# Two moves in a two-layer conv and attention kernel: which engine evicts q and k in the first part, and when the banded conv weights are zeroed

## The chip, the cores and the metric

The kernel runs on one core of one Trainium2 chip. The metric is the device time of one execution in microseconds (us). The time before is the median of three runs; the profile is of one further execution.

## The reference, cut to what matters

The input x is (2, 256, 64, 64): two images of 256 channels, 4096 tokens each. Two layers follow each other.

```python
# layer 0: attention over all 4096 tokens, 8 heads of 32 channels
q, k, v = proj(Wq, bq) / sqrt(32), proj(Wk, bk), proj(Wv, bv)   # 1x1 convolutions
attn = softmax(q @ k.T); fuse = attn @ v
x = conv1x1(concat([x, fuse]), Wf, bf) * m + x * (1 - m)        # m: mask, resized
# layer 1: channel gate, attention in 8x8 windows, two grouped 7x7 convolutions as a gate
x = x * sigmoid(relu(x @ ca_w1 + ca_b1) @ ca_w2 + ca_b2)
x = x + window_attention(x)
x = shuffle(x)                                                   # channels of 4 groups interleaved
y = relu(bn1(conv7x7(x, sa_w1)))                                 # 64 groups of 4 channels
y = bn2(conv7x7(y, sa_w2))
return x * sigmoid(y)
```

## The kernel before, in words

The program has three parts.

**The first part** (L366 to L512) makes q, k and v of all 16 chunks (2 images by 8 chunks of 512 tokens) and writes them to DRAM. A first loop (L420) takes a chunk at a time: TensorE makes q and then k, each a PSUM pair of two banks of 128 x 512 (L432, three such pairs in rotation). Each bank is read twice. VectorE adds the bias into an SBUF tile, `qst` or `kst` (L442), and ScalarE writes the square of the same sum to `sq` (L443). SyncE's queue stores `qst` and `kst` to DRAM (L447, L450); each of these tiles has two buffers. VectorE then takes the maximum over groups of four tokens of the squares (`top4`, L451), and TensorE sums them over the channels of a head one chunk later (`nrm`, L412), from which a flag is made that chooses between two versions of the attention. A second loop (L464) makes v of each chunk, ScalarE evicts it (L477), and GpSimd's queue stores it (L482).

Beside these loops runs `prepare`, a generator that the first part steps once per chunk. It builds the mask and the folded weights of the two convolutions on VectorE and, at its end, fills `w_s` with zeros: `w_s` is a DRAM tensor of 16 groups by 128 rows by 1792 floats (896 KB a group), and each group is one transfer on GpSimd's queue from a zeroed SBUF tile (L327), four of them to a step.

**The attention** (`pipeline`, L521) goes through 1024 slots in an order written out by hand: image, chunk of queries, group of four heads, block of 128 keys. In a slot TensorE makes four score tiles (L630) of the slot two ahead and four products with v (L659), ScalarE takes exponentials (L640), and VectorE adds the 128 x 2048 exponentials to a running sum for the denominators (L661). k and v come back from DRAM in pieces of four slots on SyncE's queue (`ka`, L557; `va`, L559), asked for two pieces ahead into three buffers. After each chunk of queries a generator `stage` (L718) does the rest of layer 0 and layer 1's window attention in small steps, one every fourth slot, and ends with stores of its rows to a DRAM tensor `x_s` on GpSimd's queue (L976).

`bands` (L338) is a third generator. It writes the weights' rows from two small DRAM tensors (`r1_s`, `r2_s`) into the diagonals of the zeroed `w_s`, in 156 small transfers on GpSimd's queue (L347, L353, L361), one each sixth slot. The slots only fix where these stand in the order of GpSimd's queue. Nothing in that queue waits for the attention before the first stores of `x_s`, so GpSimd issues what stands ahead of them as fast as its own waits for earlier transfers let it.

**The convolutions** (`convolve`) read `w_s` (from the last chunk of queries on) and `x_s`, and write the output.

Of the kernel before, what the change touches and what calls it, by code (L numbers as in the profile page):

```python
# [10 lines left out]
F32 = mybir.dt.float32  # L11
I32 = mybir.dt.int32
AF = mybir.ActivationFunctionType
# [6 lines left out]
P = 128  # L20
KC = C // P
# [25 lines left out]
NU = NG // UG  # L47
UW = UG * KS
# [7 lines left out]
def conv_seq_kernel(ctx: ExitStack, tc: tile.TileContext, a, out):  # L56
    nc = tc.nc
    const = ctx.enter_context(tc.tile_pool(name="const", bufs=1))
    dram = ctx.enter_context(tc.tile_pool(name="dram", bufs=1, space=bass.MemoryType.DRAM))
# [11 lines left out]
    def psum2(name):  # L71
        return ps["pair"].tile([P, 2, CH], F32, tag="s", name=name)

    def psum1(name):
        return ps["one"].tile([P, CH], F32, tag="h", name=name)
# [50 lines left out]
    w_s = dram.tile([NU, P, 2 * 32 * UW], F32, name="ws")  # L126
# [29 lines left out]
    for h in range(2):  # L156
        pending.append((cb1[64 * h : 64 * h + 64], a["ca_b1"]))
        pending.append((cw2[64 * h : 64 * h + 64], a["ca_w2"]))

    r1_s = dram.tile([32 + 4, NU, UW], F32, name="r1s")  # L160
    r2_s = dram.tile([32 + 4, NU, 4, UW // 4], F32, name="r2s")

# [2 lines left out]
    def prepare(mk, cwp):  # L165
# [55 lines left out]
        zero = cwp.tile([P, 2 * 32 * UW], F32, name="zero")  # L221
# [50 lines left out]
        for name, t in (  # L272
# [4 lines left out]
            g, beta, mean, var, cbias = (t[:, :, i] for i in range(5))  # L277
# [28 lines left out]
        for i in range(4):  # L306
            h, k = i % 2, i // 2
# [15 lines left out]
        nc.gpsimd.dma_start(  # L323
            r2_s.rearrange("p u i f -> p (u i f)"), m2.rearrange("p u i q x -> p (u i q x)")
        )
        for u in range(NU):
            nc.gpsimd.dma_start(w_s[u], zero)  # L327
            if u % 4 == 3:
                yield

    def spread(row, n):
        f = row.shape[-1]
        return row.rearrange("p u f -> u p f").to_broadcast([NU, n, f])


    def bands():  # L338
        band1 = w_s.rearrange("u p (m f) -> u (p m) f", f=UW)
        band2 = w_s.rearrange("u p (m f) -> u (p m) f", f=UW // 4)  # L340
        for q in range(4):
            for dy in range(KS):
                r0, r1 = max(0, dy - PAD), min(RB, RB + dy - PAD)
                p0, m0, n = 32 * q + 1 + r0, 1 + r0 - dy + PAD, r1 - r0
                k = KS * q + dy
                at0, step = p0 * 64 + m0, 64 + 1
                nc.gpsimd.dma_start(  # L347
                    band1[:, at0 : at0 + step * (n - 1) + 1 : step, :], spread(r1_s[k : k + 1], n)
                )
                yield  # L350
                for i in range(4):
                    at0, step = p0 * 256 + 128 + i * 32 + m0, 256 + 1
                    nc.gpsimd.dma_start(  # L353
                        band2[:, at0 : at0 + step * (n - 1) + 1 : step, :],
                        spread(r2_s[k : k + 1, :, i], n),
                    )
                    yield
            for i in range(4):
                at0 = 32 * q * 256 + 128 + i * 32 + 1
                nc.gpsimd.dma_start(  # L360
                    band2[:, at0 : at0 + RB, :], spread(r2_s[32 + q : 33 + q, :, i], RB)  # L361
                )
                yield
# [5 lines left out]
    with (  # L369
# [8 lines left out]
        for n in ("WqT", "WkT", "WvT"):  # L378
            t = w0.tile([P, KC, C], F32, name=n)
# [3 lines left out]
        bias = {}  # L383
        for n in ("bq", "bk"):
            t = w0.tile([P, KC], F32, name=n)
# [11 lines left out]
        def load_chunk():  # L397
            if len(xs0) == len(chunks):
                return
            b, c = chunks[len(xs0)]  # L400
            x = x0.tile([P, KC, CH], F32, name=f"x0_{b}_{c}")
            src = a["x"][b].rearrange("(k p) h w -> p k (h w)", p=P)
            nc.sync.dma_start(x, src[:, :, c * CH : (c + 1) * CH])
            xs0.append(x)
# [3 lines left out]
        def norms(i, tops):  # L408
            s = psum1(f"nrm_{i}")
            for n in range(2 * KC):  # L410
                s_ = s[32 * n : 32 * n + 32, 0 : CH // 4]
                nc.tensor.matmul(s_, headsum, tops[:, n, :], start=True, stop=True)  # L412
            nc.vector.tensor_reduce(nm[:, i : i + 1], s[:, 0 : CH // 4], AX.X, ALU.max)

        prepared = prepare(mk, cwp)
        next(prepared)
        for _ in range(3):
            load_chunk()
        last = None
        for i, (b, c) in enumerate(chunks):  # L420
            load_chunk()
            x = xs0[i]
            sq = st0.tile([P, 2 * KC, CH], F32, tag="sq", name=f"sq_{b}_{c}")
            tops = st0.tile([P, 2 * KC, CH // 4], F32, tag="top4", name=f"top4_{b}_{c}")
            for n, w in (("q", wq), ("k", wk)):
                s = psum2(f"{n}0_{b}_{c}")
                for g in range(KC):
                    for kc in range(KC):
                        rhs = x[:, kc, :]
                        if n == "q":  # L430
                            rhs = rhs.rearrange("p (r w c) -> p w r c", r=WS, w=NW)
                        nc.tensor.matmul(  # L432
                            s[:, g, :],
                            w[:, kc, g * P : (g + 1) * P],
                            rhs,
                            start=(kc == 0),
                            stop=(kc == KC - 1),
                        )
                t = st0.tile([P, KC, CH], F32, tag=n, name=f"{n}st_{b}_{c}")
                bt = bias["b" + n]  # L440
                for g in range(KC):
                    nc.vector.tensor_scalar_add(t[:, g, :], s[:, g, :], bt[:, g : g + 1])  # L442
                    nc.scalar.activation(  # L443
                        sq[:, g + KC * (n == "k"), :], s[:, g, :], AF.Square, bias=bt[:, g : g + 1]
                    )
                if n == "q":
                    nc.sync.dma_start(q_s[b, c], t.rearrange("p g n -> p (g n)"))  # L447
                else:
                    for g in range(KC):
                        nc.sync.dma_start(k_s[b, g, c], t[:, g, :])  # L450
            nc.vector.tensor_reduce(  # L451
                tops, sq.rearrange("p g (n f) -> p g n f", f=4), AX.X, ALU.max
            )
            if i:
                norms(i - 1, last)
            last = tops
            for t, src in pending[4 * i : 4 * i + 4]:
                nc.scalar.dma_start(t, src)
            next(prepared, None)
# [4 lines left out]
        for i, (b, c) in enumerate(chunks):  # L464
            s = psum2(f"v0_{b}_{c}")
# [30 lines left out]
            elif i == 2:  # L496


                s = psum1("bvf")
# [21 lines left out]
    def pipeline(arm, shifted, pools):  # L521
# [25 lines left out]
        def at(delay, action):  # L547
            later.append((now[0] + delay, action))

        def load_piece(n):  # L550
            if n * PB >= len(slots):
                return
            b, c, g, m = slots[n * PB]
            p = m // PB
            nm_ = f"{arm}_{b}_{c}_{g}_{p}"
            k = kvp.tile([P, PB * P], F32, tag="k", name=f"k{nm_}")
            nc.sync.dma_start(k, k_s[b, g, p])  # L557
            v = kvp.tile([P, PB, P], F32, tag="v", name=f"v{nm_}")
            nc.sync.dma_start(v, v_s[b, g, p].rearrange("p (m d) -> p m d", m=PB))  # L559
            kts[b, c, g, p], vts[b, c, g, p] = k, v  # L560

        def load_q(b, c):
            q = qp.tile([P, KC, CH], F32, tag="q", name=f"q{arm}_{b}_{c}")
            nc.sync.dma_start(q, q_s[b, c].rearrange("p (g n) -> p g n", g=KC))
            qts[b, c] = q
# [571 lines left out]
        def run_later():  # L1137
            for _ in range(len(later)):
                due, action = later.popleft()
                if due <= now[0]:  # L1140
                    action()
                else:
                    later.append((due, action))
# [8 lines left out]
        banded = bands()  # L1152
# [8 lines left out]
        for i, (b, c, g, m) in enumerate(slots):  # L1161
            now[0] = i
            if (b, c, g, m) == (B - 1, NCHUNK - 1, 0, 0):
                conv = convolve()
                next(conv)
            if m % PB == 0:
                load_piece(i // PB + AHEAD)
            if g == KC - 1 and m == 0:
                nxt = (b, c + 1) if c + 1 < NCHUNK else (b + 1, 0)
                if nxt[0] < B:  # L1170
                    load_q(*nxt)
            rest = scores(i + 2) if i + 2 < len(slots) else None
            products(i)
            if rest:
                rest()
            if g == KC - 1 and m == NMB - 1:
                at(DN + 5, lambda b=b, c=c: stages.append(stage(b, c)))
            run_later()
            if i % 6 == 1:
                next(banded, None)  # L1180
            if i % 4 == 0:
                run_stages()
# [102 lines left out]
```

## Time and profile before

| what | us |
|---|---|
| median of three runs | 3063.85 (3060.79 to 3065.46) |
| the profiled execution, its own time | 3056.05 |
| its span in the profile | 3054.1 |
| TensorE busy | 2973.5 |
| VectorE busy | 2543.1 |
| ScalarE busy | 2449.0 |
| GpSimd busy | 358.5 |

The span starts with the first instruction. In it the first part takes the first 218 us, the attention runs from there to about 2810 us, and the convolutions take the rest. A busy share is a mean over these three; what an edit is worth has to be read from the stage that it is in. In lines of the profile PE is TensorE, PEld its weight load, DVE is VectorE, ACT ScalarE, POOL GpSimd and SP SyncE; a "q" behind an engine marks the DMA issues of its queue, `q0` is the DMA queue that GpSimd's issues feed, and `q1` that of SyncE's.

### The profile page before, as it was taken

The numbers are of one execution on the slowest core, as the hardware profiler recorded it, in microseconds if no ns is written. First come the engines' busy times: TensorE is split into PE (matmuls) and PEld (weight loads), VectorE is DVE, ScalarE is ACT, GpSimd is POOL, SyncE is SP. The second block draws the span as 40 slices with busy tenths as digits, with TensorE's granted clock in tenths as the row PEclk, the third lists the DMA queues.
The fourth block names the chain that finished last, engine by engine and source line by source line (L and its number), as shares of the span: only waits on it lengthen the run. The fifth ranks groups of instructions, "written<-read, shape, count | busy, mean of one in ns | idle before, by whom it ended". The sixth has DMA issues, their size and how long they took to land.

```text
span 3054.1 us, 60829 instructions
## 1 busy us (share of the span) xinstructions
PE 2973.5 (97%) x25114; PEld 1007.6 (33%) x25114; DVE 2543.1 (83%) x1411; ACT 2449.0 (80%) x4115; POOL 358.5 (12%) x617
## 2 busy tenths in 40 slices
PE   8899989999999999999999999999999999999997
PEld 3372222232322222222222222222222222233675
DVE  5519989999999999898999998999999998999111
ACT  2239979898989899898989898989898998988333
POOL 8130000001010101010100001010101010000256
PEclk9999999999999999999999999999999999999998
DMA  7854212324242424242322324232424242413364
GB/s 214 322 176 79 63 51 63 68 60 73 62 77 60 67 73 73 66 67 74 62 72 60 66 60 73 60 74 60 75 65 70 67 70 71 105 57 106 99 196 106
DMA packets 158703, 264.19 MB, mean 87 GB/s; under 512 B 44424, under 2 KB 63068, under 8 KB 158416
## 3 DMA queue, kind: packets, MB, share of 16 engines
q1 hardware_dynamic: 129056, 213.33, 25.3%
q0 software_dynamic: 24800, 44.16, 9.3%
q8 instruction: 200, 3.28, 0.5%
q10 hardware_dynamic: 4560, 2.70, 0.3%
q14 instruction: 87, 0.71, 0.1%
HBM read 197.89 MB, written 65.21 MB: 86 GB/s over the span
## 4 chain that ended last, share of the span: by engine, by line
PE 82%; DVE 6%; ACT 2%; DMA 2%; POOL 1%; issue 0%; SPq 0%; DVEq 0%
PE sa L630 34%; PE ava L659 31%; DVE suma L661 5%; PE qka L800 4%; PE hya L729 4%; PE c2a L1064 2%; PE vwa L886 2%; PE opa L950 2%; PE c1a L1040 1%; ACT ea L640 1%; POOL out_dram L1096 1%; PE sca L834 1%; PE rda L697 1%; PE ca2a L772 1%; PE pta L909 1%; PE oa L928 1%
## 5 line engine op out<-in xcount | busy, mean ns | idle before, releaser
L661 DVE TENSOR_TENSOR suma<-suma,ea 128x2048 f32<-128x2048 f32 x960 | 2198.5, 2290 | 86.8 <-ACT ea L640 3.9
L640 ACT ACTIVATE ea<-sa 128x512 f32<-128x512 f32 (+1 forms) x3072 | 2043.9, 745 | 85.6 <-PE sa L630 40.2
L630 PE MATMUL sa<-qa,ka 32*128 32x512 f32 x8192 | 1185.7, 640 | 4.8 <-DMA ka<-ks 3.4
L659 PE MATMUL ava<-ea,va 128*32 128x512 f32 x8192 | 1092.5, 605 | 0.3 <-ACT fa L669 0.3
L630 PEld LDWEIGHTS sa<-qa,ka 32*128 32x128 f32 x8192 | 330.2, 183 | 758.2 <-ACT ea L640 687.6
L659 PEld LDWEIGHTS ava<-ea,va 128*32 128x32 f32 x8192 | 161.6, 108 | 780.8 <-issue 753.8
L976 POOL DMA_DIRECT2D xs<-xo x94 | 65.9, 708 | 2334.3 <-DVE xo L961 2333.4
L800 PE MATMUL qka<-ua,qkv_w 128*128 128x512 f32 x256 | 118.4, 605 | 0.0
L1096 POOL DMA_DIRECT2D out_dram<-za x186 | 104.6, 570 | 106.0 <-DVE za L1086 62.8
L661 DVE TENSOR_TENSOR suma<-ea,ea 128x2048 f32<-128x2048 f32 x32 | 73.1, 2284 | 51.3 <-DMA ws<-r2s 51.3
L1086 DVE TENSOR_TENSOR za<-za,xla 128x1536 f32<-128x1536 f32 (+1 forms) x16 | 22.5, 1409 | 108.1 <-ACT za L1080 70.8
L1064 PE MATMUL c2a<-yca,wa 32*128 32x192 f32 (+1 forms) x1288 | 97.6, 444 | 4.1 <-ACT za L1074 3.6
L737 ACT ACTIVATE ta<-hya,bf 128x512 f32<-128x512 f32 x32 | 20.2, 684 | 96.8 <-PE hya L729 96.8
L1074 ACT ACTIVATE za<-c2a 128x384 f32<-128x384 f32 (+1 forms) x46 | 25.9, 614 | 87.5 <-DMA out_dram<-za 59.5
L1064 PEld LDWEIGHTS c2a<-yca,wa 32*128 32x128 f32 x1288 | 88.7, 314 | 14.7 <-issue 9.9
L741 DVE TENSOR_TENSOR ta<-ta,mca 128x512 f32<-128x512 f32 x32 | 22.0, 688 | 83.2 <-ACT ta L737 83.2
L855 ACT ACTIVATE ewa<-ewa,mxwa 128x64 f32<-128x64 f32 x256 | 85.5, 362 | 1.5 <-DVE mxwa L846 1.5
L443 ACT ACTIVATE sq<-q,bq 128x512 f32<-128x512 f32 x32 | 22.0, 687 | 76.5 <-DVE qst L442 73.2
L353 POOL DMA_DIRECT2D ws<-r2s x112 | 69.5, 623 | 76.8 <-DMA xs<-xo 42.8
L813 ACT ACTIVATE qka<-qka,qkv_b 128x512 f32<-128x512 f32 x64 | 40.7, 694 | 41.6 <-PE qka L800 41.6
L432 PE MATMUL q<-x,WqT 128*128 128x512 f32 x128 | 64.1, 647 | 5.7 <-DMA WqT<-in_WqT_dram 5.7
L800 PEld LDWEIGHTS qka<-ua,qkv_w 128*128 128x128 f32 x256 | 46.0, 189 | 71.3 <-issue 58.7
(140 smaller groups left out, 1655.9 us busy)
## 6 DMA issues: line engine op xcount, KB each, us to landing
ka<-ks SPq DMA_DIRECT2D x256, 256.0 KB
va<-vs SPq DMA_DIRECT2D x256, 256.0 KB
ws<-zero POOLq DMA_DIRECT2D x16, 896.0 KB, 23.2
wa<-ws SPq DMA_DIRECT2D x16, 896.0 KB
xs<-xo POOLq DMA_DIRECT2D x78, 140.0 KB, 7.8
xla<-xs SPq DMA_DIRECT2D x25, 420.0 KB
x<-in_x_dram SPq DMA_DIRECT2D x16, 512.0 KB
qs<-qst SPq DMA_DIRECT2D x16, 512.0 KB
```

Of the source, the lines that this page charges most:

```text
L353: nc.gpsimd.dma_start(band2[:, at0 : at0 + step * (n - 1) + 1 : step, :], spread(r2_s[k : k + 1, :, i], n),)
L432: nc.tensor.matmul(s[:, g, :], w[:, kc, g * P : (g + 1) * P], rhs, start=(kc == 0), stop=(kc == KC - 1),)
L630: nc.tensor.matmul(heads[j], k[r, cols], q[r, g, :], start=True, stop=not shifted)
L640: nc.scalar.activation(e[:, h, :], tile, AF.Exp, scale=SCALE0)
L659: nc.tensor.matmul(av[r, :], v[:, m % PB, r], e[:, j, :], start=start, stop=stop)
L661: nc.vector.tensor_add(total, first[0] if m == 1 else total, e)
L729: nc.tensor.matmul(s[:, oc, :], wf[:, kc, oc * P : (oc + 1) * P], f[:, kc - KC, :] if half else xw[kc], start=(kc == 0), stop=(kc == 2 * K ...
L800: nc.tensor.matmul(s[:, j, :], wqkv[:, kc, o : o + P], u[:, kc, :], start=(kc == 0), stop=(kc == KC - 1),)
L855: nc.scalar.activation(e[:, n, :], e[:, n, :], AF.Exp, bias=mx[:, n : n + 1], accum_out=rs[:, n : n + 1],)
L976: eng.dma_start(x_s[b, n, p + r0 : p + r1].rearrange("r g w -> g r w"), xo[64 * h : 64 * h + 64, oc, r0 - WS * c : r1 - WS * c, :],)
L1064: nc.tensor.matmul(tiles[j // 2][:, j % 2, 0 : n * W], w[r, d], y[r, 0:n, d : d + W], start=(d == 0), stop=(d == KS - 1),)
L1096: engines[stores % len(engines)].dma_start(dst[b, i, r0:r1, UG * u : UG * u + UG, :], z[p + r0 : p + r1, :, nb * m + n, :],)
```

## The change

- In the first part ScalarE alone evicts q and k: two activations with the bias write the tile, and a third squares the whole 128 x 1024 tile from SBUF. VectorE's additions go.
- `prepare` writes the zeros once, to a DRAM tensor `zero_s` of 896 KB. Its sixteen transfers to `w_s` go, and with them three of its steps.
- `bands` begins with sixteen transfers from `zero_s` to the groups of `w_s`, one to a step, from DRAM to DRAM, on GpSimd's queue.
- `bands` is stepped each fifth slot instead of each sixth, and what is left of it would be issued at the slot where the convolutions are set up. It has 172 steps, and 5 times 172 is 860, so at that slot, 960, nothing is left.

```diff
+    zero_s = dram.tile([P, 2 * 32 * UW], F32, name="zeros")
...
-        for u in range(NU):
-            nc.gpsimd.dma_start(w_s[u], zero)
-            if u % 4 == 3:
-                yield
+        nc.gpsimd.dma_start(zero_s, zero)
+        yield
...
     def bands():
         band1 = w_s.rearrange("u p (m f) -> u (p m) f", f=UW)
         band2 = w_s.rearrange("u p (m f) -> u (p m) f", f=UW // 4)
+        for u in range(NU):
+            nc.gpsimd.dma_start(w_s[u], zero_s)
+            yield
...
                 for g in range(KC):
-                    nc.vector.tensor_scalar_add(t[:, g, :], s[:, g, :], bt[:, g : g + 1])
                     nc.scalar.activation(
-                        sq[:, g + KC * (n == "k"), :], s[:, g, :], AF.Square, bias=bt[:, g : g + 1]
-                    )
+                        t[:, g, :], s[:, g, :], AF.Identity, bias=bt[:, g : g + 1]
+                    )
+                nc.scalar.activation(sq[:, 0:KC] if n == "q" else sq[:, KC:], t, AF.Square)
...
             if (b, c, g, m) == (B - 1, NCHUNK - 1, 0, 0):
+                for _ in banded:
+                    pass
                 conv = convolve()
...
-            if i % 6 == 1:
+            if i % 5 == 1:
                 next(banded, None)
```

## The prediction, made before the changed kernel was run

> **What bounds the kernel now.** I read the windows by stage first, then the waits and the timeline of the first part, then the start of the attention. From 400 to 2700 us TensorE is busy over 99% of the time; the change adds no compute there. The two ends of interest lie before 245 us.
>
> ```profile
> core 0: us, PE busy (x) PEld busy (x) DVE busy (x) ACT busy (x) POOL busy (x), PEclk, DMA share, GB/s
> ...
> 60.00:100.00 40.00, 35.08 (x104) 14.25 (x104) 28.73 (x55) 13.86 (x22) 13.11 (x23) 0.96 0.56 186
> 100.00:140.00 40.00, 32.70 (x98) 12.99 (x96) 22.78 (x29) 10.94 (x16) 9.02 (x17) 0.96 0.95 374
> 140.00:180.00 40.00, 33.88 (x136) 23.47 (x137) 13.06 (x20) 9.90 (x13) 4.29 (x8) 0.83 0.73 283
> ```
>
> TensorE idles most where the DMA share is highest (100 to 140), and its granted clock falls to 0.83 afterwards. ScalarE is idle two thirds of the time. Why, the timeline of one chunk shows:
>
> ```profile
> 64.75 0.73 DVE L442 TENSOR_SCALAR qst<-q,bq 128x512 f32<-128x512 f32 x1
> ...
> 65.58 0.69 ACT L443 ACTIVATE sq<-q,bq 128x512 f32<-128x512 f32 x1 [0.34 <-DVE qst L442]
> ...
> 66.30 0.75 DVE L442 TENSOR_SCALAR qst<-q,bq 128x512 f32<-128x512 f32 x1 [0.82 <-ACT sq L443]
> ...
> 67.09 0.69 ACT L443 ACTIVATE sq<-q,bq 128x512 f32<-128x512 f32 x1 [0.82 <-DVE qst L442]
> ...
> 69.97 2.29 DVE L451 TENSOR_REDUCE top<-sq 128x512 f32<-128x2048 f32 x1 [0.75 <-ACT sq L443]
> ```
>
> VectorE and ScalarE take turns on the same PSUM tile: one chunk's loop is 7.4 us of such turns with `top4`, then `nm` 0.28 and whatever `prepare` puts on VectorE. TensorE waits for its end:
>
> ```profile
> ACT sq L443 <- DVE qst L442: 73.2, 30, 7.0
> ...
> PE nrm L412 <- DVE top L451: 15.4, 12, 4.0
> ...
> DVE qst L442 <- DMA qs<-qst: 6.7, 2, 3.6
> ```
>
> The last of these is the zeros: from 103 to about 142 us `ws<-zero` fills the DMA engines, and stores issued at 112 us free their tile only at 129. In that stretch the two queues get exactly one packet each in turn:
>
> ```profile
> q0 software_dynamic: 394, 2.54, 78.6%
> q1 hardware_dynamic: 387, 0.71, 23.7%
> ```
>
> (128 to 136 us: packets, MB, share of 16 engines.) The zeros' packets are 7168 B and SyncE's about 2 KB, so SyncE's queue gets 0.71 of 3.25 MB. Last, the start of the attention:
>
> ```profile
> 219.82 0.67 POOL L347 DMA_DIRECT2D ws<-r1s  x1 [0.47 <-issue]
> ...
> 221.88 0.38 SPq L570 DMA_DIRECT2D xa<-in_x_dram  x1
> 222.39 0.39 SPq L573 DMA_DIRECT2D mca<-masks  x1
> 222.90 2.07 SPq L557 DMA_DIRECT2D ka<-ks  x1
> ...
> 237.69 1.14 PE L630 MATMUL sa<-qa,ka 32*128 32x512 f32 x8 [3.36 <-DMA ka<-ks]
> ```
>
> GpSimd has left the first part and issues bands at once, unpaced by the slots. x waits for the last v store; the third piece of k (call it ka2) stands behind x (512 KB) and the mask (256 KB) on SyncE's queue and needs 14.8 us; TensorE waits 3.4 us for it. **Whatever the change puts at the head of the bands lands exactly here.**
>
> **What the Trainium skill says.** "PSUM — Partial Sum Buffer", PSUM bank collisions: two engines may not touch one bank and quadrant at once, reads included, and are kept apart by a dependency. The trace agrees: the turns above. "DMA: Bandwidth & Descriptors", Queues, rings and completion order: a DMA engine goes round its queue rows packet by packet. Agrees: 394 against 387. The same page, Why a DMA increments its semaphore by 16: a contiguous one-dimensional access is split in an outer dimension of a multiple of 16 so that it spreads over the engines. No transfer of the kernel before has this form.
>
> **The change, part by part.** *Evictions.* Per chunk VectorE loses four additions of 0.74, and the turns go. ScalarE does four Identities (the 128x512 Square with bias took 0.69; the Identity of L737 684 ns) and two Squares of 128x1024 without bias: the skill's "ScalarE: Activation LUTs", What ACT_TABLE_LOAD costs, gives 186 ns + 0.833 ns an element, 1.04 us; the 1024-wide copy L477 took 1.01. I take 1.04: ScalarE 4 x 0.69 + 2 x 1.04 = 4.8 us a chunk, under TensorE's time. VectorE is left with 2.29 + 0.28 and at most 4 us of `prepare` (72.4 to 76.1): 6.6. So TensorE sets the pace: chunks that waited for nothing started at 23.42, 30.84 and 38.42, that is 7.4 to 7.6. I take 7.5. Before, the 14 chunks from 23.42 to the first v at 156.03 took 132.6 us; after, 14 x 7.5 = 105.0: **27.6 saved**. About half of it is the last two chunks (125.74 to 156.03, 30.3 where 15 would do), which are slow by the zeros' stores and the clock that falls with each stall. The v loop took 156.03 to 218.05, 62.0; sixteen chunks at the 3.45 of its undisturbed end are 55.2, `nrm`, the flag and `bvf` 1.5, and a wait of 1.2 for the last `top4` (0.69 x 2 + 1.04 + 2.29 against 3.5 of v): 57.9, **4.1 saved**. Together 31.7. Bounds: 22 if a turn of 0.7 us remains in each chunk, 34 if none of the 1.2 is seen. The one zero transfer left in the first part (896 KB, some 2.3 us of 16 engines by the 403 GB/s below) hides under 7.5 us chunks at about 210 GB/s.
>
> *Zeros in the attention.* Sixteen transfers of 917,504 B, 14.68 MB. GpSimd issues them at once (before, nine went out in 4.83 us, the others as earlier ones landed), 2 us ahead of x. From SBUF they ran at 403 GB/s (14.75 MB in 66.6% of 55 us). From DRAM to DRAM no row exists; the skill's DMA page, Latency and other measured facts, gives 214 GB/s each way for copies between DRAM tensors. Bounds 403 and 214; I take 214, since read and write both go to DRAM: an estimate of 68.6 us. Both sides are contiguous, so by the sentence above each of 16 engines gets one packet of 57,344 B a transfer, 4.29 us each. The alternative is 128 rows of 7168 B, as before.
>
> With 57 KB packets SyncE's queue gets one 2 KB packet per engine between two of them. x needs 16 per engine, the mask 8, ka2 8. Sixteen are passed by the time all sixteen zero packets are done: so ka2 comes only after the whole zeroing. Start 221, plus 68.6, plus 16 x 0.11 (307 engine-us for 2880 packets from 300 to 400 us) = 291.3; then 16 packets of mask and ka2, 1.8, and some 2 to land: 295. That matmul ran at 237.69: **57.3 lost**. Nothing hides it: k and v are held for 8 slots, 16.5 us. VectorE doesn't give it back: from 240.86 to 392.39 it does 66 additions at 2.29 without a gap, as a slot is 2.07 on TensorE, so its end moves with the stall. What is late next: some ten bands, which wait for the zeros to land and then meet ka3; 0 to 3 us, taken at 0.
>
> *Every fifth slot.* 12.8 instead of 10.7 issues a chunk of queries, 0.62 us each on GpSimd, behind the stores of `x_s`; from 1000 to 2000 us TensorE was busy 995.3 with such bursts, so 0, at most 2 if a burst meets a piece. The loop ahead of the convolutions issues nothing.
>
> Sum against the profiled execution: 3056.05 - 31.7 + 57.3 = 3081.7, **+25.6**. That execution was 7.8 below the median shown; on the median it is 3063.85 + 25.6, about **3089**.
>
> **The rivals.**
> - *57 KB packets, faster copy.* At 403 GB/s the zeroing is 36.4 us and ka2's matmul comes at 263: +25 - 32, 3057. For it: an engine may read and write at full rate. Against: the page's figure. The point at which loss equals gain is a zeroing of 43 us, 341 GB/s.
> - *The other side: 7168 B packets.* If the rows stay rows, SyncE passes one packet per zero packet of 0.54 us, 0.65 with its own. A piece (16 packets an engine) takes 10.4 where TensorE needs 8.3; zeroing takes 128 x 0.65 = 83 us, in which (128 - 24)/16 = 6.5 pieces pass. They end at 306 instead of 234.3 + 6.5 x 8.27 = 288: 18 of stall for the 3.4, +15 - 32 = -17: 3047. It decides where a zero packet stays under about 1.5 us.
> - *7168 B packets at 0.29 us*: a piece takes 6.4, less than the 8.3 needed; ka2 comes in time. -32 - 2: 3030.
> - *The evictions bring nothing*, because TensorE already waits little in light chunks: then 3056 - 15 of the zeros + 57, 3106 on the median. Against: `nrm <- top` 15.4 us.
>
> **Chances.** 57 KB packets at about 214 GB/s 0.48 (3089, its own range 3074 to 3106, the gain of 22 to 34 and the last rival within it); 57 KB and faster 0.22 (3052 to 3072); rows, slow 0.20; rows, fast 0.10. The range 3038 to 3106 leaves out the last and the outer ends. A measurement here tells about 0.2%, 6 us, from no change. Faster: 0.08 + 0.19 + 0.10 = 0.37; same 0.08 + 0.01 = 0.09; slower 0.48 + 0.06 = 0.54.
>
> **What would show it.** Right: `ACT sq <- DVE qst` gone, chunks 7.5 us apart, the first v near 128 us, the attention near 186; then a stretch of some 55 us at its start with TensorE idle, its matmul waiting for `ka<-ks`, the DMA full, few packets on q0 and hardly any on q1. Packets of 7 KB on q0 there would make the second rival true; a zeroing under 43 us the first; chunks still 8.5 apart the last.

## The result, and the profile after

| | before | after |
|---|---|---|
| median, 20 runs each (us) | 3062.24 (3055.48 to 3068.66) | 3066.91 (3062.12 to 3070.04) |
| after / before | | 1.0014, 95% interval 1.0007 to 1.0022 |
| the profiled execution (us) | 3056.05 | 3066.36 |
| its span (us) | 3054.1 | 3064.6 |

The change costs 4.7 us, 0.14%: within the 0.2% that counts here as no change. It was forecast 25.6 us slower. Behind the small sum stand two large terms of opposite sign, both where the prediction put them. The stages, first the windows (columns as before: length, busy time of each engine, granted clock, DMA share, GB/s):

```profile
core 0: us, PE busy (x) PEld busy (x) DVE busy (x) ACT busy (x) POOL busy (x), PEclk, DMA share, GB/s
...
60.00:100.00 40.00, 40.00 (x135) 16.79 (x134) 18.50 (x41) 26.27 (x34) 15.28 (x27) 1.00 0.73 246
100.00:140.00 40.00, 39.15 (x151) 20.75 (x150) 13.45 (x15) 20.59 (x26) 2.15 (x4) 1.00 0.40 145
140.00:180.00 40.00, 40.00 (x191) 35.33 (x190) 0.16 (x1) 12.03 (x12) 11.77 (x22) 1.00 0.51 189
...
200.00:220.00 20.00, 3.37 (x28) 0.63 (x24) 8.79 (x4) 4.27 (x7) 2.92 (x6) 0.67 1.00 337
220.00:240.00 20.00, 0.00 (x0) 0.00 (x0) 0.00 (x0) 0.00 (x0) 0.00 (x0) 0.50 0.92 300
```

From 60 to 180 us TensorE is now busy nearly all the time at a granted clock of 1.00. From 60 to 140 us ScalarE carries about twice what it did and is still idle at least a third of the time. From 220 to 240 us no compute engine does anything, while the DMA engines are 92% busy. The waits of the first 300 us name both (in all, times, longest):

```profile
DVE top L453 <- ACT sq L447: 82.2, 16, 20.9
...
PE sa L632 <- DMA ka<-ks: 37.6, 1, 37.6
...
PE nrm L414 <- DVE top L453: 2.9, 2, 2.0
```

The 73.2 us of ScalarE waiting for `qst` are gone, VectorE now waits for work, and TensorE's wait for `top4` fell from 15.4 to 2.9. In their place is one wait of 37.6 us for a piece of k. TensorE's timeline gives the dates:

```profile
68.18 3.70 PE L434 MATMUL q<-x,WqT 128*128 128x512 f32 x8
...
75.60 3.70 PE L434 MATMUL q<-x,WqT 128*128 128x512 f32 x8
...
127.54 3.72 PE L471 MATMUL v<-WvT,x 128*128 128x256 f32 x16
...
187.12 3.06 PE L632 MATMUL sa<-qa,ka 32*128 32x512 f32 x16 [1.19 <-ACT vst L479]
```

The same two starts before:

```profile
156.03 5.99 PE L469 MATMUL v<-WvT,x 128*128 128x256 f32 x16
...
218.09 3.06 PE L630 MATMUL sa<-qa,ka 32*128 32x512 f32 x16 [1.19 <-ACT vst L477]
```

Chunks are 7.42 us apart, v starts at 127.54 instead of 156.03, and the attention's first matmul at 187.12 instead of 218.09: 31.0 us won. Then, from the timeline of all engines after:

```profile
188.82 0.53 POOL L341 DMA_DIRECT2D ws<-zeros  x1 [0.44 <-issue]
...
191.13 0.38 SPq L572 DMA_DIRECT2D xa<-in_x_dram  x1
...
192.77 0.42 SPq L559 DMA_DIRECT2D ka<-ks  x1
...
217.04 0.49 POOL L341 DMA_DIRECT2D ws<-zeros  x1 [2.75 <-DMA ws<-zeros]
240.93 2.09 PE L632 MATMUL sa<-qa,ka 32*128 32x512 f32 x8 [37.56 <-DMA ka<-ks]
```

The zeros go out 2.3 us ahead of x and 4 us ahead of ka2; the matmul that needs ka2 runs at 240.93. From the attention's start that is 53.8 us, where it was 19.6: 34.2 us lost. 34.2 - 31.0 = 3.2 of the medians' 4.7. The two profiled spans differ by more, 10.5. VectorE takes a reciprocal of the denominators once a chunk of queries: at the first one the kernel after is 3.8 behind (396.17 against 392.39), at the seventh 2.2 (1377.00 against 1374.80), at the last 7.6 (2834.46 against 2826.83). 3.3 of this came in the eighth chunk, which takes 166.4 us instead of the usual 163.2, with TensorE's weight load waiting for nothing that the profile names. The last 2.9 arise behind the last reciprocal. What causes either is open. Before's executions spread over 13 us, and its profiled one lies at their low end.

### The profile page after: what moved, and what is told of

Same layout as the page of the kernel before. It is cut to its first block, busy times and chain, and to the rows that moved or that the text cites. A ratio compares the mean times of both kernels' runs of the same rounds, so it can differ in the third digit from the quotient of the medians.

```text
span 3064.6 us, 60799 instructions
## 1 busy us (share of the span) xinstructions
PE 2965.6 (97%) x25114; PEld 1006.8 (33%) x25114; DVE 2497.7 (82%) x1347; ACT 2478.4 (81%) x4147; POOL 358.4 (12%) x618
## 4 chain that ended last, share of the span: by engine, by line
PE 77%; DVE 9%; DMA 3%; issue 2%; ACT 2%; SPq 1%; POOL 1%; DVEq 0%; ACTq 0%
PE sa L632 31%; PE ava L661 29%; DVE suma L663 8%; PE qka L802 4%; PE hya L731 4%; PE vwa L888 2%; DMA ka<-ks 2%; PE c2a L1066 2%; PE opa L952 1%; PE c1a L1042 1%; ACT ea L642 1%; PE rda L699 1%; PE sca L836 1%; PE ca2a L774 1%; PE pta L911 1%
## 5 line engine op out<-in xcount | busy, mean ns | idle before, releaser
L632 PE MATMUL sa<-qa,ka 32*128 32x512 f32 x8192 | 1185.3, 640 | 39.0 <-DMA ka<-ks 37.6
L453 DVE TENSOR_REDUCE top<-sq 128x512 f32<-128x2048 f32 x16 | 36.6, 2286 | 82.2 <-ACT sq L447 82.2
```

The costliest lines, as they stand in the source:

```text
L632: nc.tensor.matmul(heads[j], k[r, cols], q[r, g, :], start=True, stop=not shifted)
```

## The experiments

The theory after the result: the first part wins 31 us, 19 of them by the evictions; the start of the attention loses 34 because packets of 57 KB take turns one for one with SyncE's packets of 2 KB (a turn is one packet of one queue on one DMA engine). The main rival for the loss: the DMA engines are simply full until 14.7 MB have passed. The main rival for the gain: it all comes from the zeros' departure from the first part. In the tables below "before" is the median of the runs of the kernel before on the same chip.

### The two halves apart

`e1_evict_only` has only the evictions of the change:

```diff
-                    nc.vector.tensor_scalar_add(t[:, g, :], s[:, g, :], bt[:, g : g + 1])
                     nc.scalar.activation(
-                        sq[:, g + KC * (n == "k"), :], s[:, g, :], AF.Square, bias=bt[:, g : g + 1]
+                        t[:, g, :], s[:, g, :], AF.Identity, bias=bt[:, g : g + 1]
                     )
+                nc.scalar.activation(sq[:, 0:KC] if n == "q" else sq[:, KC:], t, AF.Square)
```

Expected: 

> Only the evictions are changed; the zeros stay in the first part, from SBUF. Theory (31 us won in the first part, 34 lost at the attention's start): the light chunks run at 7.4 us, but the zeros' 7 KB packets still take turns with the stores, so the stall of some 12 us at chunks 12 to 15 stays; the attention starts near 199 us and waits 3.4 us for ka as before: 3062 - 19 = 3043. Rival (the evictions bring nothing, the first part's gain is all from the zeros' departure): 3062, attention at 218.

`e2_zeros_only` is the change without these lines, so it moves the zeros and steps `bands` each fifth slot. Expected: 

> Only the zeros are moved; VectorE and ScalarE evict by turns as before. Theory: the first part wins the 15 us of its last chunks, the attention loses 34: 3062 + 19 = 3081, attention near 203 us, wait for ka 37 us. Rival (evictions bring nothing): the same as the whole change, 3067.

| | median | before | ratio (interval) | attention starts | wait for ka |
|---|---|---|---|---|---|
| evictions only | 3041.98 | 3060.96 | 0.9936 (0.9914 to 0.9958) | 199.37 | 1.8 |
| zeros only | 3085.36 | 3060.96 | 1.0066 (1.0044 to 1.0087) | 205.14 | 38.4 |

-19.0 and +24.4 add up to +5.4, the whole change's +4.7 within the runs' spread. The evictions are worth 19 by themselves, so the rival for the gain is out; the zeros' departure wins 13.0 in the first part and costs 35 later (259.83 - 205.14 = 54.7 against 19.6). The window of the evictions-only kernel in which the zeros still pass shows what it leaves:

```profile
100.00:140.00 40.00, 31.83 (x98) 14.02 (x97) 9.87 (x8) 16.72 (x22) 3.11 (x6) 0.92 1.02 412
```

DMA full, TensorE idle for 8 us; in its waits ScalarE stands for the stores of q:

```profile
ACT qst L442 <- DMA qs<-qst: 14.2, 4, 6.3
```

### What in the evictions pays

`e7_vector_evicts` stands on the version with the zeros on SyncE's queue (below, 3024.91). VectorE evicts q and k as before, and only the square is taken from SBUF, by ScalarE:

```diff
                 for g in range(KC):
-                    nc.scalar.activation(
-                        t[:, g, :], s[:, g, :], AF.Identity, bias=bt[:, g : g + 1]
-                    )
+                    nc.vector.tensor_scalar_add(t[:, g, :], s[:, g, :], bt[:, g : g + 1])
                 nc.scalar.activation(sq[:, 0:KC] if n == "q" else sq[:, KC:], t, AF.Square)
```

Expected: 

> The run with the zeros on SyncE's queue, but VectorE evicts q and k with the bias as before, and ScalarE squares the evicted tile from SBUF. So no PSUM tile has two readers, and VectorE keeps its 3 us a chunk. Theory (the turns were what cost): VectorE has 5.5 us a chunk and only the chunks with prepare's work slip: 3025 + 5 = 3030, first v near 132 us. Rival (VectorE's load was what cost): chunks stay 8.5 to 9 us apart, first v near 141 as with the zeros alone moved: 3039.

Measured: 3029.00, before 3061.86, ratio 0.9893 (0.9868 to 0.9919). Its chunks on TensorE:

```profile
61.14 3.70 PE L434 MATMUL q<-x,WqT 128*128 128x512 f32 x8
68.56 3.70 PE L434 MATMUL q<-x,WqT 128*128 128x512 f32 x8
...
129.22 3.72 PE L469 MATMUL v<-WvT,x 128*128 128x256 f32 x16
```

7.42 apart, except for 8.4 and 7.7 after them, where `prepare` has its reciprocals; v starts at 129.22. VectorE keeps its additions, some 2.8 us a chunk, and v starts 1.6 us later than with ScalarE alone (127.63 in the run that this one stands on). With two readers, in the zeros-only run, it starts here:

```profile
141.17 3.72 PE L471 MATMUL v<-WvT,x 128*128 128x256 f32 x16
```

12 of 13.5 us are won without ScalarE's eviction, and 16.2 of 17.9 at the attention's start (205.14 with two readers, 188.95 with VectorE alone, 187.22 with ScalarE alone). So what paid was that a PSUM tile has one reader and not two; which of the two it is matters little: the intervals of this run and of the one that it stands on overlap. ScalarE's squares also fall from 2.8 to 2.1 us a chunk in this run. As ScalarE was idle two thirds of the time, that is an unlikely cause, but no run tries it alone.

### The size of a packet

Bytes, queue and place stay; only the cut of the zero transfers changes:

```diff
-            nc.gpsimd.dma_start(w_s[u], zero_s)
+            nc.gpsimd.dma_start(w_s[u], zero_s, max_dma_last_dim=7168)
```

`e3_rows_7k`, expected: 

> The whole change, with each zero transfer cut into packets of 7168 B instead of 57344 B; bytes, place and queue are the same. Theory (the packets' size starves SyncE's queue, one packet each in turn): a zero packet takes 0.35 us and a packet of SyncE's 0.11, so ka2 comes 32 turns of 0.46, 15 us, after the start, some 4 late, va2 a little later, and then a piece takes 7.4 of the 8.3 us it has: wait for ka about 6 us, 3062 - 27 = 3035. Rival (the DMA engines are simply full: 14.7 MB have to pass first): wait for ka 37 us as in the whole change, 3067.

`e4_rows_2k`, the same with 2048, expected: 

> As the run with 7168 B packets, with packets of 2048 B. Theory of turns: a zero packet and one of SyncE's take about 0.15 and 0.11 us, ka2 comes 32 turns, 8 us, after the start, in time: no wait for ka, 3062 - 31 - 3 = 3028. Rival (bytes decide): wait 37 us, 3067. What may fall short: more packets cost more in all, so the zeroing lasts up to 115 us; on this theory that costs nothing.

| packet | median | before | ratio (interval) | wait for ka | matmul with ka2 |
|---|---|---|---|---|---|
| 57,344 B (the change) | 3066.91 | 3062.24 | 1.0014 (1.0007 to 1.0022) | 37.6 | 240.93 |
| 7168 B | 3033.54 | 3060.96 | 0.9904 (0.9874 to 0.9935) | 8.7 | 212.63 |
| 2048 B | 3036.00 | 3061.86 | 0.9912 (0.9880 to 0.9943) | 4.3 | 207.81 |

One number in the code is worth 33 us, and the DMA engines are as full as before (353 to 375 GB/s from 210 to 240 us with 7168 B). The rival "simply full" is out. The queues side by side, the whole change from 200 to 220 us:

```profile
DMA packets 443, 6.73 MB, mean 337 GB/s; under 512 B 125, under 2 KB 125, under 8 KB 333
...
q0 software_dynamic: 221, 6.31, 91.4%
q1 hardware_dynamic: 222, 0.43, 9.0%
```

and with 7168 B, from 210 to 220:

```profile
q0 software_dynamic: 459, 2.90, 76.4%
q1 hardware_dynamic: 464, 0.85, 24.1%
```

(Packets, MB, share of 16 engines.) Both times packet for packet, 222 to 221 and 464 to 459. But a turn moves 2 KB on one side and what the packet holds on the other: SyncE's queue gets 22 GB/s in the first and 85 in the second, and the pieces of k and v need 63 (512 KB in 4 slots, 8.27 us). The 2048 B run was slower than expected: ka2 still waited 4.3, and some 8 more us came in single long chunks of queries after 360 us (164.7, 165.3 and 168.2 for 163.2 in its trace), of the kind told above and as little explained. The intervals of the two runs overlap, so which of the two sizes is better isn't shown.

### How many of SyncE's packets pass

The first fence above holds a detail that the prediction lacked. 443 - 333 = 110 packets are over 8 KB; q0's 6.31 MB are on them, 57 KB each. The other 111 of q0's 221 packets are tiny, one to each large one. I take them for completion packets, with which each engine reports its share of a transfer as done; the profile doesn't name them. They take a turn too, so two packets of SyncE's pass per engine and transfer, 222 to 110. Two runs test this count.

`e8_x_late` asks for the first x and mask at slot 8, behind the pieces:

```diff
-        load_x(0, 0)
...
             if m % PB == 0:
                 load_piece(i // PB + AHEAD)
+            if i == 8:
+                load_x(0, 0)
```

Expected: 

> The whole change with x and the mask of the first chunk asked for at slot 8, behind the pieces of k and v, instead of ahead of them. Theory (two packets of SyncE's per engine and zero transfer): ka2 is 8 packets behind, 4 transfers or 11 us, and comes in time; the 32 packets of the zeroing are two pieces, so TensorE gets 8 slots, 16.5 us, further before it waits: 3067 - 16 = 3051, wait for ka and va about 20 us in all. Rival (bytes decide, ahead of everything): no change, 3067.

Measured: 3046.75, before 3061.86, ratio 0.9943 (0.9929 to 0.9958), a little better than expected. TensorE's waits (the trace is of the longest of its twelve runs, 3053.53):

```profile
215.51 2.09 PE L632 MATMUL sa<-qa,ka 32*128 32x512 f32 x8 [3.26 <-DMA ka<-ks]
...
227.12 1.24 PE L661 MATMUL ava<-ea,va 128*32 128x512 f32 x8 [3.72 <-DMA va<-vs]
...
239.26 2.09 PE L632 MATMUL sa<-qa,ka 32*128 32x512 f32 x8 [7.43 <-DMA ka<-ks]
```

ka2 comes in time, and TensorE waits 14.4 us in all for the loads behind it, where the change has one wait of 37.6. 20 us are won without moving a byte less: that much of the 34 us hung on what stood ahead of ka2 in its queue.

`e6_double` doubles the suspected cost:

```diff
+    w2_s = dram.tile([NU, P, 2 * 32 * UW], F32, name="ws2")
...
             nc.gpsimd.dma_start(w_s[u], zero_s)
+            nc.gpsimd.dma_start(w2_s[u], zero_s)
```

Expected: 

> The whole change with every zero transfer done twice, the second to a scratch tensor that nobody reads (16 more transfers, 14.7 MB). The trace of the whole change shows two packets of SyncE's per engine and zero transfer, one beside its data packet and one beside its small completion packet, and about 2.8 us a transfer. Theory: ka2, 32 packets behind, still comes after 16 transfers, 45 us; in the next 45 us 32 packets pass, two pieces, 16.5 us of TensorE's work: 28 us more, 3067 + 28 = 3095. Rivals: copies at 214 GB/s would add 52; if SyncE's queue got nothing at all until the zeros are done, 45: 3112.

Measured: 3095.92, before 3061.86, ratio 1.0115 (1.0082 to 1.0147). It is 29.0 over the whole change; 28 was expected from two packets a transfer, 45 if SyncE's queue got nothing until the zeros are done, 52 at 214 GB/s. Its waits:

```profile
249.70 2.09 PE L634 MATMUL sa<-qa,ka 32*128 32x512 f32 x8 [46.20 <-DMA ka<-ks]
...
261.20 1.94 PE L663 MATMUL ava<-ea,va 128*32 128x512 f32 x8 [4.48 <-DMA va<-vs]
...
275.34 2.09 PE L634 MATMUL sa<-qa,ka 32*128 32x512 f32 x8 [8.32 <-DMA ka<-ks]
```

ka2 itself comes 9 us later than in the change, where the same time was expected: the sum of the run was foretold better than its first wait. The count of turns had left out that x, the mask and ka2, 512 packets of data, have small packets of their own. In the change 441 of SyncE's packets had passed by 235 us, and 490 more passed in the next 5 us as the zeros ended. Here the zeros go on, 478 had passed by 240 us, and the rest still had to take turns.

### A version that beats both

`e5_sync_queue`: 57 KB packets, on the queue that they starved.

```diff
-            nc.gpsimd.dma_start(w_s[u], zero_s)
+            nc.sync.dma_start(w_s[u], zero_s)
```

Expected: 

> The whole change, with the zero transfers on SyncE's queue instead of GpSimd's. There they stand between the loads of k and v, which wait for free buffers, so one goes out each fifth slot. Theory: each delays a piece by its 2.8 us, within the two pieces of lead; no stall at the start, and the bands no longer start at once: 3062 - 31 - 3 = 3028. Rival (the zeroing costs its bytes wherever it lies in the attention): 3062 - 31 + 34 = 3065.

Measured: 3024.91, before 3060.96, ratio 0.9869 (0.9839 to 0.9899): 36 us faster, and the trace has no wait for ka in the first 330 us. SyncE's queue:

```profile
199.77 1.12 SPq L341 DMA_DIRECT2D ws<-zeros  x1
202.58 0.33 SPq L559 DMA_DIRECT2D ka<-ks  x1
207.71 0.32 SPq L561 DMA_DIRECT2D va<-vs  x1
208.08 0.47 SPq L341 DMA_DIRECT2D ws<-zeros  x1
```

Here the loads wait for free buffers, so the place in the order of slots is also a place in time, and the delay of one zero transfer (an estimate from 917,504 B at the 345 GB/s of the change: 2.7 us) falls within the lead of two pieces. On GpSimd's queue "every fifth slot" was a place in the order only; all sixteen left in 29 us. The bands, which wait for the zeros, now begin at 375.33 us instead of 241.10, clear of the start.

## Why the prediction was right and wrong, by its own steps

- **The evictions and the first part: right.** 31.7 won was forecast, 31.0 came: chunks 7.5 apart against 7.42, first v "near 128" against 127.54, the attention "near 186" against 187.12. The sum is in part luck: the chunks won 28.5 for 27.6, the v loop 2.5 for 4.1. That the two readers' turns were the cause is now shown by the run in which VectorE evicts alone. The Trainium skill's "PSUM — Partial Sum Buffer", PSUM bank collisions, explains only part of these turns, since it keeps two engines apart on one bank and quadrant. The tile here has two banks, and in the prediction's own lines VectorE's read of the second (66.30) waits 0.82 us for ScalarE's read of the first. This wait follows the whole tile and not the bank. Two tiles of one bank each were not tried.
- **Place, form and mechanism of the loss: right.** Eight issues within some 4 us, the first 2.3 us ahead of x, and the others as earlier ones landed; one packet of 57 KB per engine and transfer; turns packet for packet; ka2 only at the end of the zeroing.
- **The step that failed: "From DRAM to DRAM no row exists ... I take 214".** The term of 68.6 us for the zeroing was mis-sized. The trace has 6.31 MB in 91.4% of 20 us, 345 GB/s while q0 moved (2.66 us a packet, not 4.29); with 7168 B packets 2.90 MB in 76.4% of 10 us, 380. Sixteen of 2.66 are 42.6 us; 32 packets of SyncE's at 0.13 (9.0% of 20 us, 16 engines, 222 packets) add 4.2: 46.8 from the first to the last, and 34.2 lost instead of 57.3. With 2.66 for 4.29 the prediction's own sum gives 31.2 lost, and with 16 more packets at 0.13 it gives 33.3, so the rate is the error that counts. The prediction had 341 GB/s as the point at which loss equals gain; the copy runs at nearly that rate, which is why the two terms nearly cancel. The figure of 214 in the Trainium skill's "DMA: Bandwidth & Descriptors", Latency and other measured facts, is for rows of 16 KiB on the sync and scalar queues; taking it as the rate of this copy was the error, and both bounds were on the table.
- **The count of turns: wrong, without effect here.** The prediction let 16 packets pass on each engine during the zeroing and 16 after it. Two passed per transfer, since the small packets take turns too: 441 over 16 engines, some 28 each, by 235 us. Either way ka2 came at the end.
- **VectorE gives nothing back: right, on a loose reading.** "66 additions at 2.29 without a gap" are 63 in the trace, some 2.39 apart, behind gaps of 0.79 and 1.28 us. TensorE is 3.2 us behind at ka2, and the first reciprocal 3.8.
- **Every fifth slot at 0: not tried apart.** No run isolates it; the runs with it show no new wait for k or v past the start in the windows that I read. Beyond the first, chunks of queries longer than 164 us stand in six of the eight traces with every fifth slot and in neither of the two with every sixth. One trace of each kernel can't tell whether that is the cause.
- **The rivals.** "57 KB packets, faster copy" is what came: 3066.91 lies in its 3052 to 3072. 7168 B packets were priced at 3047 at 214 GB/s and 3030 at 403; the run gave 3033.54, the value of the faster copy. "The evictions bring nothing" fell with the evictions-only run.

## What to carry to other kernels

Two queues shared a DMA engine here by packets, not by bytes (222 to 221 packets, 0.43 to 6.31 MB): a bulk copy in packets of 57 KB on one queue starved loads in 2 KB packets on the other, and cutting the packets to 7 KB or putting the bulk between the loads on the same queue gave back 33 and 42 us. A transfer placed "at slot n" is paced only if its queue waits for something that runs with the slots: GpSimd's sixteen left in 29 us, SyncE's one by one. Where a sum has two large terms of opposite sign, price both from rows measured on the same kind of transfer: here the choice between two bounds decided the sign.

## What the runs showed of the hardware that I had not expected

- Copies between DRAM tensors ran at 345 GB/s in 57 KB packets and 380 in 7168 B packets, over the time in which their queue moved data (the same bytes from SBUF, in 7168 B packets: 403).
- Beside each large packet went a tiny one, which I take for its completion packet, and it took a turn of its own against the other queue: two packets of SyncE's per zero transfer and engine, 222 against 110 data packets.
- Two readers of a PSUM tile on two engines, in the program's order, cost 16 to 18 us up to the attention's start (205.14 against 188.95 and 187.22), though neither engine was busy more than three quarters of the time.
